# Block normalisation among the last six expert runs, and row-wise correction of the last four

## Chip, cores and metric

One core of one Trainium2 chip. Its engines run side by side, each through its own queue in program order: PE (matmul, with PEld for its weight loads), DVE (vector), ACT (activation functions), POOL (general, and the only issuer of row-indexed, that is indirect, DMAs here) and SP (issues plain DMAs). The metric is device time in microseconds. Three runs of the kernel before took 1161.5, 1162.44 and 1162.81 us; the median, 1162.44 us, is the time before.

## What is computed

The input is 32 sequences of 128 tokens, 256 wide (4096 tokens). A cross-attention with 16 heads is added to the tokens, then a mixture-of-experts layer: each token goes to the two best of eight experts, their results are weighed and summed, and a layer norm with gamma and beta is taken of token plus sum.

```python
    x = x + xattn(layernorm(x), ctx_768, ...)
    n = layernorm(x)
    # ffn(n):
    logits = n @ Wg + bg
    top2_vals, top2_idx = top_k(logits, 2)
    scores = softmax(top2_vals)
    y_e = gelu(n @ W1[e] + b1[e]) @ W2[e] + b2[e]
    out = sum over the two chosen e of scores_e * y_e
    x = x + layer_norm(n + out) * gamma + beta
```

## The kernel before

Everything is fp32. The tokens are eight blocks of 512. Attention runs block by block; `norm_gate` then writes a block's normed rows to DRAM twice: to `xrows`, from which the experts fetch, and to `total`, to which they add. Attention ends near 640 us of the span.

The expert layer is 43 runs (`MAIN`), each over 256 or 128 slots of one expert: 25 long and 18 short ones. A run's slots are tokens in order of their block, so early long runs hold tokens of early blocks. A list, `order`, says which run comes when: six long runs of tokens of the first four blocks (`AHEAD`, `OLD`), then short and long runs in turn, then two long runs (numbers 41 and 42) that hold no token of the first four blocks. A run m consists of

- `fetch_who(m)` (six runs ahead), `fetch_rows(m)` (four ahead, on POOL, one indirect gather for each 128 rows) and `fetch_weights(m)` (two ahead, on SP: W1 of 1 MB, a bias row, W2 of 1 MB, into one of three buffers);
- `turn(m)`: PE transposes the rows, DVE copies them out of PSUM;
- `hidden(m)`: eight times two matmuls (line 448), each pair followed on ACT by a Gelu (line 451);
- `outputs(m)`: for each 128 rows eight matmuls (line 466), two DVE steps (474 adds the bias, 475 multiplies by the score), and on POOL an indirect DMA that adds the rows to `total` (line 478). Such an add waits until the adds of the run before have landed.

In the loop PE works in the order hidden(m), turn(m+1), outputs(m-1). All results in PSUM, of whatever kind, take turns in eight banks. After run 40's first half stands a branch over three spare runs, which are not needed with these inputs (line 1179 waits for the register that decides it).

Then the ending. `outputs(40)`, the two transposes, and on SP the loads of the first four blocks' sums (line 1103) are issued; `hidden(41)`, `hidden(42)`, `outputs(41)`, `outputs(42)` follow. Those loads wait until run 40's add has landed; `declare_no_dep` with the list `early` keeps the adds of runs 41 and 42 from waiting for the loads. A block's norm is `measure` (DVE, four times lines 147 and 148, then 153, and a power on POOL, line 154), `scale` (a small DVE step, line 1129, then four activations on ACT, line 1131), `multiply` by gamma, which was copied to PSUM (line 1139), `add_residual` (line 1143) and `store`. Blocks 0 to 3 are normed beside the last two runs. Blocks 4 to 7 are loaded once run 42's adds have landed, and normed then. For two of them the residual was stored to the output earlier (line 1093), and the norm is added to it by DMA (line 1150).

Of the kernel before, what the change touches and what calls it, by code (L numbers as in the profile page):

```python
# [10 lines left out]
F32 = mybir.dt.float32  # L11
# [5 lines left out]
P = 128  # L17
# [8 lines left out]
def kernel(  # L26
# [38 lines left out]
    NPART = (2 * NTOK - NFULL * 256) // P + NE - 1  # L65


    OLD = NBLK // 2
    EARLY = (2 * OLD * TOK - NE) // 256 + NE


    AHEAD = 6
    assert AHEAD <= (2 * OLD * TOK - NE * 255 + 255) // 256
    SLOTS = 12 * CAP

# [36 lines left out]
    slots = dram.tile([SLOTS, 2], U32, name="slots")  # L112
    xrows = dram.tile([NTOK + P, D], F32, name="xrows")
    total = dram.tile([NTOK + P, D], F32, name="total")

    BW = NHC + D
    biases = dram.tile([NE, P, BW], F32, name="biases")
# [32 lines left out]
    def deviation(pool, mv, rstd):  # L150

        ve = pool.tile([P, TB], F32, name="ve", tag="ve")
        nc.vector.tensor_scalar_add(ve, mv[:, :, 1], LN_EPS)  # L153
        nc.gpsimd.tensor_tensor(rstd, ve, mhalf, ALU.pow)  # L154
# [298 lines left out]
                then()  # L453
        hiddens[m] = hT

    added, early = [], []

    def outputs(m, then=None):

        nt, who, hT = order[m][2], whos.pop(m), hiddens.pop(m)  # L460
        mine = []
        w1t, bt, w2t = weights.pop(m)
        for t in range(nt):
            py = flat(bank("py"))
            for c in range(NHC):
                nc.tensor.matmul(  # L466
                    py[:, :D],
                    lhsT=hT[c // (NHC // 2)][:, c % (NHC // 2), ts(t, P)],
                    rhs=w2t[:, c, :],
                    start=(c == 0),  # L470
                    stop=(c == NHC - 1),
                )
            y = f3.tile([P, D], F32, name=f"y{m}_{t}", tag="y")
            nc.vector.tensor_tensor(y, py[:, :D], bt[:, NHC:], ALU.add)  # L474
            nc.vector.tensor_scalar(y, y, who[:, t, 1:2].bitcast(F32), None, ALU.mult)  # L475
            if t > 0:
                nc.gpsimd.memset(apart, 0.0)
            add = nc.gpsimd.indirect_dma_start(  # L478
                out=reach(total, m),
                out_offset=bass.IndirectOffsetOnAxis(ap=who[:, t, 0:1], axis=0),  # L480
                in_=y,
                in_offset=None,
                compute_op=ALU.add,
            )


            for other in mine:
                tc.declare_no_dep(add.ins, other.ins, reason="tokens of their own")
            for other in added:
                tc.add_manual_dep(add.ins, other.ins.name, DATA, reason="the run before")  # L490
            if MAIN - 2 <= m < MAIN:
                for other in early:
                    tc.declare_no_dep(add.ins, other.ins, reason="no tokens of the first blocks")
            mine.append(add)
            if t == 0 and then is not None:
                then()
        added[:] = mine
# [583 lines left out]
    ADDED = (OLD, OLD + 1)  # L1081
# [12 lines left out]

    def load_sums(blk, n=1):

        tag = ("qT", "xnT", "rows", "wkm", "wvm")[blk // 2 if blk < 6 else blk - 3]
        acc = (a2 if blk < 6 else aw).tile([P, TB, D], F32, name=f"acc{blk}", tag=tag)
        accs[blk] = acc
        loads = []  # L1100
        for i in range(n):
            own = slice(blk * TOK + i * TOK // n, blk * TOK + (i + 1) * TOK // n)
            got = nc.sync.dma_start(  # L1103
                out=acc[:, ts(i, TB // n), :], in_=total[own, :].rearrange("(t s) d -> s t d", s=S)
            )
            for other in added:
                tc.add_manual_dep(got.ins, other.ins.name, DATA, reason="these sums are complete")
            loads.append(got)
        return loads

    def measure(blk, tiles=range(TB)):

        if blk not in scales:
            scales[blk] = (
                fs.tile([P, TB, 2], F32, name="mv3", tag="mv3"),
                fs.tile([P, TB], F32, name="rstd3", tag="rstd3"),
            )
        mv, rstd = scales[blk]
        for t in tiles:
            tile_stats(fs, accs[blk], mv, t)  # L1120
        if TB - 1 in tiles:
            deviation(fs, mv, rstd)

    def scale(blk):

# [9 lines left out]
    def multiply(blk, tiles=slice(0, TB)):  # L1135

        piece = accs[blk][:, tiles, :]
        w = piece.shape[1]
        nc.vector.tensor_tensor(piece, piece, factors[0].unsqueeze(1).to_broadcast([P, w, D]), ALU.mult)  # L1139

    def add_residual(blk, tiles=slice(0, TB)):
        piece = accs[blk][:, tiles, :]
        nc.vector.tensor_tensor(piece, piece, xres[blk][:, tiles, :], ALU.add)  # L1143

    def store(blk, tiles=slice(0, TB)):
        nc.sync.dma_start(out=of_block(out, blk)[:, tiles, :], in_=accs[blk][:, tiles, :])

    def send(blk):

        add = nc.gpsimd.dma_start(out=of_block(out, blk), in_=accs.pop(blk), accum_op=ALU.add)  # L1150
        tc.add_manual_dep(add.ins, stored[blk].ins.name, DATA, reason="the residual first")

    L = MAIN - 1
    pending = AHEAD - 1
    for m in range(AHEAD, L - 1):
        if m == L - 4:
# [10 lines left out]
        if m == L - 3:  # L1167
# [36 lines left out]
    measure(2)  # L1204
    scale(1)

    def third():
        measure(3)
        scale(2)

    def second():
        multiply(1)
        scale(3)
        multiply(2)

    outputs(L - 1, third)
    multiply(0)
    outputs(L, second)
    multiply(3)
    for blk in range(2):  # L1220
        add_residual(blk)
        store(blk)
    for blk in range(OLD, NBLK):
        load_sums(blk, TB if blk == OLD else 1)
    for blk in range(2, OLD):
        add_residual(blk)
        store(blk)
    measure(OLD)
    measure(OLD + 1, range(2))
    for blk in range(OLD, NBLK - 1):  # L1230
        scale(blk)
        measure(blk + 1, range(2, TB))
        if blk + 2 < NBLK:
            measure(blk + 2, range(2))
        multiply(blk)
        if blk in ADDED:
            send(blk)
    scale(last)
    add_residual(last - 1)
    store(last - 1)  # L1240
    for h in range(2):
        tiles = slice(h * TB // 2, (h + 1) * TB // 2)
        multiply(last, tiles)
        add_residual(last, tiles)
        store(last, tiles)


# [42 lines left out]
```

## Time and profile before

The profiled execution took 1161.17 us on the device; its trace spans 1159.5 us, so 1.7 us lie around the span. It is 1.3 us below the median of the runs shown.

| Engine | busy, us | share of the span |
|---|---|---|
| PE | 1110.3 | 96% |
| PEld | 859.2 | 74% |
| DVE | 585.3 | 50% |
| ACT | 462.5 | 40% |
| POOL | 288.7 | 25% |

| Costliest pieces of the expert layer | count | us of one |
|---|---|---|
| matmul of hidden, line 448 | 1376 | 0.336 (mean of both widths) |
| matmul of outputs, line 466 | 1088 | 0.379 |
| Gelu, line 451 | 344 | 0.429 |
| indirect add to `total`, line 478 | 68 | 1.666 |
| indirect gather of rows, line 419 | 64 | 0.988 |
| power on POOL, line 154 | 24 | 1.048 |

Matmuls overlap one another, so their durations add up to more than the time they take; the distance from one to the next is read from the timeline. A share of the whole span hides that stages differ: the time is looked at stage by stage.

### The profile page before, as it was taken

The numbers are of one execution on the slowest core, as the hardware profiler recorded it, in microseconds if no ns is written. First come the engines' busy times: TensorE is split into PE (matmuls) and PEld (weight loads), VectorE is DVE, ScalarE is ACT, GpSimd is POOL, SyncE is SP. The second block draws the span as 40 slices with busy tenths as digits, with TensorE's granted clock in tenths as the row PEclk, the third lists the DMA queues.
The fourth block names the chain that finished last, engine by engine and source line by source line (L and its number), as shares of the span: only waits on it lengthen the run. The fifth ranks groups of instructions, "written<-read, shape, count | busy, mean of one in ns | idle before, by whom it ended". The sixth has DMA issues, their size and how long they took to land. (4 is left out here: it accounts for less than half of the span.)

```text
span 1159.5 us, 19043 instructions
## 1 busy us (share of the span) xinstructions
PE 1110.3 (96%) x6805; PEld 859.2 (74%) x6805; DVE 585.3 (50%) x1476; ACT 462.5 (40%) x1609; POOL 288.7 (25%) x349
## 2 busy tenths in 40 slices
PE   7999999999999999999899999999999999999980
PEld 4666767676667676766668888899899898898870
DVE  4876685867867868678457361122211111111166
ACT  2565363544543635445244222333332332332252
POOL 1000012030030020300402563434433433433242
PEclk9999999999999999999899999999999999999995
DMA  9400101110111001001124758888888888888748
GB/s 311 146 1 19 38 1 19 37 20 1 38 19 38 1 2 37 2 1 39 19 78 133 224 111 271 245 248 239 261 241 259 240 243 244 266 247 259 203 107 220
DMA packets 124608, 148.59 MB, mean 128 GB/s; under 512 B 21536, under 2 KB 110048, under 8 KB 124512
## 3 DMA queue, kind: packets, MB, share of 16 engines
q1 hardware_dynamic: 107360, 127.35, 34.2%
q0 software_dynamic: 16160, 18.95, 8.8%
q8 instruction: 55, 0.90, 0.3%
q10 hardware_dynamic: 992, 1.05, 0.3%
q14 instruction: 41, 0.34, 0.1%
HBM read 122.97 MB, written 24.35 MB: 127 GB/s over the span
## 5 line engine op out<-in xcount | busy, mean ns | idle before, releaser
L451 ACT ACTIVATE hT<-ph,b 128x256 f32<-128x256 f32 (+1 forms) x344 | 146.4, 429 | 343.1 <-PE ph L448 306.0
L721 ACT ACTIVATE pr<-pss,nmax 128x128 f32<-128x128 f32 x512 | 179.2, 401 | 227.0 <-DVE nmax L717 215.8
L448 PE MATMUL ph<-xT,w 128*128 128x256 f32 (+1 forms) x1376 | 244.1, 336 | 0.6 <-DVE xT L436 0.6
L466 PE MATMUL py<-w,hT 128*128 128x256 f32 x1088 | 242.1, 379 | 1.0 <-DVEq L1179 1.0
L448 PEld LDWEIGHTS ph<-xT,w 128*128 128x128 f32 x1376 | 218.9, 191 | 22.5 <-DVE xT L436 0.9
L466 PEld LDWEIGHTS py<-w,hT 128*128 128x128 f32 x1088 | 203.4, 190 | 27.3 <-issue 1.4
L478 POOL DMA_INDIRECT total<-y,who x68 | 113.3, 1666 | 254.1 <-DVE y L475 173.6
L721 ACT ACTIVATION_READ_ACCUMULATOR pr<-pss,nmax 128x1 f32 x512 | 124.0, 242 | 0.0
L474 DVE TENSOR_TENSOR y<-py,b 128x256 f32<-128x256 f32 x68 | 28.9, 424 | 176.6 <-PE py L466 176.6
L686 PE MATMUL pq<-xnT,wq_sb 128*128 128x512 f32 x256 | 115.2, 592 | 0.3 <-DVE xnT L609 0.3
L780 PE MATMUL pw<-wo_sb,oT 128*128 128x256 f32 x512 | 113.3, 379 | 0.0
L436 DVE COPY xT<-px 128x512 f32<-128x512 f32 (+1 forms) x43 | 24.8, 578 | 169.0 <-PE px L434 165.7
L780 PEld LDWEIGHTS pw<-wo_sb,oT 128*128 128x128 f32 x512 | 96.0, 190 | 12.6 <-issue 0.2
L154 POOL TENSOR_TENSOR rstd<-ve,mhalf 128x4 f32<-128x4 f32 x24 | 25.1, 1048 | 282.5 <-DVE ve L153 279.4
L686 PEld LDWEIGHTS pq<-xnT,wq_sb 128*128 128x128 f32 x256 | 48.6, 190 | 61.3 <-issue 57.3
L128 POOL DMA_INDIRECT slots<-info,ati x64 | 62.8, 981 | 113.6 <-DVE ati L915 95.4
L735 DVE TENSOR_TENSOR pr<-pr,rden 128x512 f32<-128x512 f32 x128 | 88.5, 692 | 4.4
L717 DVE TENSOR_REDUCE nmax<-pss 128x4 f32<-128x512 f32 x128 | 79.4, 683 | 16.2 <-PE pss L707 16.2
L707 PE MATMUL pss<-kT,qT 64*128 64x128 f32 x1024 | 69.7, 282 | 5.3 <-issue 5.2
L707 PEld LDWEIGHTS pss<-kT,qT 64*128 64x128 f32 x1024 | 62.5, 190 | 12.5 <-issue 12.1
L745 PEld LDWEIGHTS ptp<-ident,pr 128*128 128x128 f32 x512 | 57.8, 141 | 17.0 <-issue 16.1
L419 POOL DMA_INDIRECT xg<-xrows,who x64 | 63.3, 988 | 22.5 <-issue 13.2
(164 smaller groups left out, 1147.1 us busy)
## 6 DMA issues: line engine op xcount, KB each, us to landing
w<-in_L_ffn_W_dram SPq DMA_DIRECT2D x86, 1024.0 KB
b<-biases SPq DMA_DIRECT2D x43, 132.0 KB
xres<-in_x_dram SPq DMA_DIRECT2D x8, 512.0 KB
xrows<-rows SPq DMA_DIRECT2D x8, 512.0 KB
total<-rows SPq DMA_DIRECT2D x8, 512.0 KB
acc<-total SPq DMA_DIRECT2D x7, 512.0 KB
ctx<-in_ctx_dram SPq DMA_DIRECT2D x8, 384.0 KB
out_dram<-acc SPq DMA_DIRECT2D x5, 512.0 KB
```

The source lines that it names most:

```text
L128: s = nc.gpsimd.indirect_dma_start(out=slots, out_offset=bass.IndirectOffsetOnAxis(ap=at, axis=0), in_=info, in_offset=None)
L419: nc.gpsimd.indirect_dma_start(out=xg[:, t, :], out_offset=None, in_=reach(xrows, m), in_offset=bass.IndirectOffsetOnAxis(ap=whos[m][:, t, ...
L448: nc.tensor.matmul(ph[:, : nt * P], lhsT=w1t[:, k, ts(c, P)], rhs=xT[:, k, :], start=(k == 0), stop=(k == KD - 1))
L451: nc.scalar.activation(hT[c // half][:, c % half, :], ph[:, : nt * P], AF.Gelu, bias=bt[:, c : c + 1])
L466: nc.tensor.matmul(py[:, :D], lhsT=hT[c // (NHC // 2)][:, c % (NHC // 2), ts(t, P)], rhs=w2t[:, c, :], start=(c == 0), stop=(c == NHC - 1),)
L478: add = nc.gpsimd.indirect_dma_start(out=reach(total, m), out_offset=bass.IndirectOffsetOnAxis(ap=who[:, t, 0:1], axis=0), in_=y, in_offse ...
L686: nc.tensor.matmul(pq, lhsT=wq_sb[:, k, ts(2 * q + c, P)], rhs=xnTs[blk][:, k, :], start=(k == 0), stop=(k == KD - 1),)
L707: nc.tensor.matmul(pss[2 * c + h][:, t, :], lhsT=qT[ts(h, DH), c, ts(t, S)], rhs=kT[ts(h, DH), c, ts(t, S)], start=True, stop=True,)
L717: nc.vector.tensor_reduce(nmax, pss[h], AX.X, ALU.max, negate=True)
L721: nc.scalar.activation(pr[:, t, :], pss[h][:, t, :], AF.Exp, bias=nmax[:, t : t + 1], accum_out=den[:, t : t + 1],)
L735: nc.vector.tensor_tensor(pr, pr, rden.unsqueeze(2).to_broadcast([P, TB, S]), ALU.mult)
L780: nc.tensor.matmul(pw[:, :D], lhsT=oTs[blk][:, k, ts(t, S)], rhs=wo_sb[:, k, :], start=(k == 0), stop=(k == NHP - 1),)
```

## The change

- `OLD` goes from 4 to 3 and `AHEAD` from 6 to 5. With these the list of runs becomes: five long runs, then 18 short and 14 long ones, then six long runs (37 to 42) without tokens of the first three blocks. The number of runs and their sizes stay. At the start of the mixed stretch two short runs precede each long one three times (runs 5 to 13).
- `fetch_rows(5)` and later ones move behind other steps, since run 5 is now one of the runs that the second table lists.
- Every block's residual (with beta) is stored to a new DRAM tensor `resid` (line 1093's place), where before two blocks' went to the output.
- The branch stands before run 37's first half. From run 37 (`X`) on PE works in the order hidden(m), turn(m+1), outputs(m).
- The sums of blocks 0 to 2 are loaded once run 36's add has landed, and those blocks are normed beside runs 37 to 39. The declaration with `early` is gone.
- The rows of `resid` that belong to the tokens of runs 39 to 42 are gathered on POOL (`fetch_own(bases, ...)`, eight indirect DMAs) beside run 38.
- The sums of blocks 3 to 7 are loaded once run 38's adds have landed, and normed and stored beside runs 39 to 42, still without the contributions of these runs.
- Runs 39 to 42 use `last_outputs`: the sums of the run's own tokens are gathered from `total` when the scatters of the run before have landed; DVE adds the run's result to them; the new sums are scattered over the rows of `total` (a plain write; not for run 42). `patch` norms these rows, multiplies by gamma and adds the residual rows; `send` scatters them over the stored rows of the output, after the stores of blocks 3 to 7 and after the rows of the run before.
- Gamma is read from SBUF instead of PSUM; `multiply`, `add_residual` and `store` become `by_gamma` and `put_out`.

```diff
-    OLD = NBLK // 2
+    OLD = 3
     EARLY = (2 * OLD * TOK - NE) // 256 + NE
...
-    AHEAD = 6
+    AHEAD = 5
...
+    resid = dram.tile([NTOK, D], F32, name="resid")
...
                 tc.add_manual_dep(add.ins, other.ins.name, DATA, reason="the run before")
-            if MAIN - 2 <= m < MAIN:
-                for other in early:
-                    tc.declare_no_dep(add.ins, other.ins, reason="no tokens of the first blocks")
...
     fetch_weights(2)
     norm_gate(last)
     fetch_rows(4)
-    fetch_rows(5)
...
     turn(4)
+    fetch_rows(5)
     outputs(2)
     fetch_weights(5)
     fetch_rows(6)
-    fetch_rows(7)
     hidden(4)
...
     fetch_weights(6)
+    fetch_rows(7)
     fetch_rows(8)
-    fetch_rows(9)
-    hidden(5)
-    turn(6)
-    outputs(4)
-    fetch_weights(7)
...
-        if blk in ADDED:
-            stored[blk] = nc.sync.dma_start(out=of_block(out, blk), in_=xres[blk])
-
-    def load_sums(blk, n=1):
+        nc.sync.dma_start(out=block(resid, blk), in_=xres[blk])
+    def load_sums(blk):
...
+        got = nc.sync.dma_start(out=acc, in_=block(total, blk))
+        for other in added:
+            tc.add_manual_dep(got.ins, other.ins.name, DATA, reason="these sums are complete")
+        return got
...
+    def by_gamma(rows):
+        w = rows.shape[1]
+        nc.vector.tensor_tensor(rows, rows, gamma_sb.unsqueeze(1).to_broadcast([P, w, D]), ALU.mult)
+    def put_out(blk):
+        acc = accs.pop(blk)
+        by_gamma(acc)
+        nc.vector.tensor_tensor(acc, acc, xres[blk], ALU.add)
+        stored[blk] = nc.sync.dma_start(out=of_block(out, blk), in_=acc)
+    PATCH = 4
     L = MAIN - 1
+    X = MAIN - (NREST - EARLY + AHEAD)
...
+    sums = aw.tile([P, PATCH, 2, D], F32, name="sums", tag="wo_sb")
+    bases = aw.tile([P, PATCH, 2, D], F32, name="bases", tag="wq_sb")
...
+    def own(t, m):
+        return t[:, m - (L - PATCH + 1)]
+    def fetch_own(t, table, m, complete=()):
+        for i in range(2):
+            got = nc.gpsimd.indirect_dma_start(
+                out=own(t, m)[:, i, :],
+                out_offset=None,
+                in_=table,
+                in_offset=bass.IndirectOffsetOnAxis(ap=whos[m][:, i, 0:1], axis=0),
+            )
+            for other in complete:
+                tc.add_manual_dep(got.ins, other.ins.name, DATA, reason="these sums are complete")
+    def last_outputs(m, then=None):
+        who, hT = whos.pop(m), hiddens.pop(m)
+        whose[m] = who
+        w1t, bt, w2t = weights.pop(m)
+        mine = []
...
+            y = f3.tile([P, D], F32, name=f"y{m}_{t}", tag="y")
+            z = own(sums, m)[:, t, :]
+            nc.vector.tensor_tensor(y, py[:, :D], bt[:, NHC:], ALU.add)
+            nc.vector.scalar_tensor_tensor(z, y, who[:, t, 1:2].bitcast(F32), z, ALU.mult, ALU.add)
+            if m < L:
+                if t > 0:
+                    nc.gpsimd.memset(apart, 0.0)
+                put = nc.gpsimd.indirect_dma_start(
+                    out=total,
+                    out_offset=bass.IndirectOffsetOnAxis(ap=who[:, t, 0:1], axis=0),
+                    in_=z,
+                    in_offset=None,
+                )
+                for other in mine:
+                    tc.declare_no_dep(put.ins, other.ins, reason="tokens of their own")
+                for other in added + loads:
+                    tc.add_manual_dep(put.ins, other.ins.name, DATA, reason="what came before")
+                mine.append(put)
+            if then is not None:
+                then(t)
+        added[:] = mine
+    def patch(m, tiles=slice(0, 2)):
+        z = own(sums, m)[:, tiles, :]
+        n = z.shape[1]
+        mv = fs.tile([P, 2, 2], F32, name="mvp", tag="mvp")
+        ve = fs.tile([P, 2], F32, name="vep", tag="vep")
+        rstd = fs.tile([P, 2], F32, name="rstdp", tag="rstdp")
+        for t in range(n):
+            tile_stats(fs, z, mv, t)
+        nc.vector.tensor_scalar_add(ve[:, :n], mv[:, :n, 1], LN_EPS)
+        nc.gpsimd.tensor_tensor(rstd[:, :n], ve[:, :n], mhalf[:, :n], ALU.pow)
+        for t in range(n):
+            nc.vector.tensor_scalar(z[:, t, :], z[:, t, :], mv[:, t, 0:1], rstd[:, t : t + 1], ALU.subtract, ALU.mult)
+        by_gamma(z)
+        nc.vector.tensor_tensor(z, z, own(bases, m)[:, tiles, :], ALU.add)
+    def send(m):
+        z = own(sums, m)
+        mine = []
...
+            put = nc.gpsimd.indirect_dma_start(
+                out=out_rows,
+                out_offset=bass.IndirectOffsetOnAxis(ap=whose[m][:, t, 0:1], axis=0),
+                in_=z[:, t, :],
+                in_offset=None,
+            )
+            for other in mine:
+                tc.declare_no_dep(put.ins, other.ins, reason="tokens of their own")
+            for other in sent + [stored[blk] for blk in range(OLD, NBLK)]:
+                tc.add_manual_dep(put.ins, other.ins.name, DATA, reason="over what came before")
+            mine.append(put)
+        sent[:] = mine
...
-        if m + WEIGHTS < L:
+        if m + WEIGHTS <= X:
             fetch_weights(m + WEIGHTS)
-        if m < L - 2:
+        if m < X - 1:
...
-    fetch_weights(L)
-    outputs(L - 2)
-    turn(L - 1)
-    turn(L)
+    fetch_weights(X + 1)
+    turn(X)
+    outputs(X - 1)
+    def run(m):
+        if m + WEIGHTS <= L:
+            fetch_weights(m + WEIGHTS)
+        if m + ROWS <= L:
+            fetch_rows(m + ROWS)
+        hidden(m)
+        if m < L:
+            turn(m + 1)
+    run(X)
     for blk in range(OLD):
-        early += load_sums(blk)
-    hidden(L - 1)
-    hidden(L)
-
-    pf = flat(bank("factors"))
-    nc.scalar.copy(pf[:, :D], gamma_sb)
-    factors = [pf[:, :D]]
-    measure(0)
-    measure(1)
-    scale(0)
-    measure(2)
+        load_sums(blk)
+    def behind_first():
+        measure(0)
+        measure(1)
+        scale(0)
+    outputs(X, behind_first)
+    for m in range(X + 1, L - PATCH):
+        run(m)
+        outputs(m)
+    for m in range(L - PATCH + 1, L + 1):
+        fetch_own(bases, resid, m)
+    m = L - PATCH
+    run(m)
+    put_out(0)
     scale(1)
 
...
+    def behind_second():
+        measure(2)
+        put_out(1)
         scale(2)
...
+    outputs(m, behind_second)
+    m = L - 3
+    fetch_weights(m + WEIGHTS)
     for blk in range(OLD, NBLK):
+        loads.append(load_sums(blk))
+    fetch_own(sums, total, m, added)
+    hidden(m)
+    turn(m + 1)
+    put_out(2)
+    measure(3)
+    def behind(t):
+        if t == 0:
+            measure(4)
+            scale(3)
+    last_outputs(m, behind)
+    put_out(3)
+    m = L - 2
+    fetch_own(sums, total, m, added)
+    fetch_weights(m + WEIGHTS)
+    hidden(m)
+    turn(m + 1)
+    measure(5)
+    scale(4)
+    measure(6)
+    scale(5)
+    put_out(4)
+    def behind(t):
+        if t == 0:
+            put_out(5)
+    last_outputs(m, behind)
+    measure(7)
+    m = L - 1
+    fetch_own(sums, total, m, added)
+    hidden(m, lambda: scale(6), 3)
+    turn(m + 1)
+    scale(7)
+    put_out(6)
+    patch(L - 3)
+    put_out(7)
+    last_outputs(m)
+    send(L - 3)
+    m = L
+    patch(L - 2)
+    fetch_own(sums, total, m, added)
+    hidden(m)
+    patch(L - 1)
+    send(L - 2)
+    def behind(t):
+        patch(L, slice(t, t + 1))
+        if t == 0:
+            send(L - 1)
+    last_outputs(m, behind)
+    send(L)
```

More of the change, by code (lines that the diff above doesn't have):

```diff
@@ L454, in hidden @@
         hiddens[m] = hT
-    added, early = [], []
+    added = []
     def outputs(m, then=None):
@@ L1071 @@
     fetch_weights(6)
+    fetch_rows(7)
     fetch_rows(8)
-    fetch_rows(9)
-    hidden(5)
-    turn(6)
-    outputs(4)
-    fetch_weights(7)
     accs, scales, stored = {}, {}, {}
-    ADDED = (OLD, OLD + 1)
     def of_block(t, blk):
@@ L1099, in load_sums, with measure @@
         accs[blk] = acc
[L1100 to L1117, printed above, removed]
+        got = nc.sync.dma_start(out=acc, in_=block(total, blk))
+        for other in added:
+            tc.add_manual_dep(got.ins, other.ins.name, DATA, reason="these sums are complete")
+        return got
+    def measure(blk):
+        scales[blk] = (
+            fs.tile([P, TB, 2], F32, name="mv3", tag="mv3"),
+            fs.tile([P, TB], F32, name="rstd3", tag="rstd3"),
+        )
         mv, rstd = scales[blk]
-        for t in tiles:
+        for t in range(TB):
             tile_stats(fs, accs[blk], mv, t)
-        if TB - 1 in tiles:
-            deviation(fs, mv, rstd)
+        deviation(fs, mv, rstd)
     def scale(blk):
@@ L1133, in scale @@
             )
[L1135 to L1146, printed above, removed]
@@ L1148, in send @@
-    def send(blk):
-        add = nc.gpsimd.dma_start(out=of_block(out, blk), in_=accs.pop(blk), accum_op=ALU.add)
-        tc.add_manual_dep(add.ins, stored[blk].ins.name, DATA, reason="the residual first")
-    L = MAIN - 1
+    def by_gamma(rows):
[6 more added lines that the diff above has]
+        stored[blk] = nc.sync.dma_start(out=of_block(out, blk), in_=acc)
@@ new lines @@
+    PATCH = 4
+    L = MAIN - 1
+    X = MAIN - (NREST - EARLY + AHEAD)
+    assert L - PATCH >= X + 1
+    out_rows = out.rearrange("b s d -> (b s) d")
+    sums = aw.tile([P, PATCH, 2, D], F32, name="sums", tag="wo_sb")
+    bases = aw.tile([P, PATCH, 2, D], F32, name="bases", tag="wq_sb")
+    whose, sent = {}, []
+    def own(t, m):
[10 more added lines that the diff above has]
+                tc.add_manual_dep(got.ins, other.ins.name, DATA, reason="these sums are complete")
@@ new lines, in last_outputs @@
+    def last_outputs(m, then=None):
[3 more added lines that the diff above has]
+        mine = []
+        for t in range(2):
+            py = flat(bank("py"))
+            for c in range(NHC):
+                nc.tensor.matmul(
+                    py[:, :D],
+                    lhsT=hT[c // (NHC // 2)][:, c % (NHC // 2), ts(t, P)],
+                    rhs=w2t[:, c, :],
+                    start=(c == 0),
+                    stop=(c == NHC - 1),
+                )
[11 more added lines that the diff above has]
+                    in_offset=None,
+                )
+                for other in mine:
[6 more added lines that the diff above has]
+        added[:] = mine
@@ new lines, in send @@
+    def send(m):
+        z = own(sums, m)
+        mine = []
+        for t in range(2):
+            if t > 0:
+                nc.gpsimd.memset(apart, 0.0)
+            put = nc.gpsimd.indirect_dma_start(
[3 more added lines that the diff above has]
+                in_offset=None,
+            )
+            for other in mine:
[4 more added lines that the diff above has]
+        sent[:] = mine
@@ L1154 @@
+    loads = []
     pending = AHEAD - 1
-    for m in range(AHEAD, L - 1):
-        if m == L - 4:
+    for m in range(AHEAD, X):
+        if m == X - 3:
             spare = nc.values_load(
@@ L1166 @@
             fetch_rows(m + ROWS)
-        if m == L - 3:
+        if m == X - 2:
             other = weights[m]
-        if m + WEIGHTS < L:
+        if m + WEIGHTS <= X:
             fetch_weights(m + WEIGHTS)
         hidden(m)
-        if m < L - 2:
+        if m < X - 1:
             turn(m + 1)
@@ L1205 @@
+    run(X)
+    for blk in range(OLD):
+        load_sums(blk)
[12 more added lines that the diff above has]
+    put_out(0)
     scale(1)
-    def third():
-        measure(3)
+    def behind_second():
+        measure(2)
+        put_out(1)
         scale(2)
[L1211 to L1222, printed above, removed]
-    for blk in range(OLD, NBLK):
[L1224 to L1245, printed above, removed]
+    outputs(m, behind_second)
+    m = L - 3
+    fetch_weights(m + WEIGHTS)
+    for blk in range(OLD, NBLK):
+        loads.append(load_sums(blk))
[8 more added lines that the diff above has]
+            scale(3)
```

## Prediction

> **What bounds the kernel now.** I read the page's slices first: PE is busy at nine tenths or more from the second slice to the 38th, so until the ending the kernel is as long as its matmuls. Then I cut the ending into stretches (columns: stretch, its length, busy time of PE, PEld, DVE, ACT, POOL with counts, granted PE clock, DMA share, GB/s):
>
> ```profile
> 1112.00:1126.60 14.60, 14.59 (x68) 12.51 (x66) 12.25 (x40) 8.77 (x18) 8.20 (x8) 1.00 0.23 45
> 1126.60:1159.50 32.90, 0.00 (x0) 0.00 (x0) 23.00 (x55) 9.00 (x18) 9.22 (x9) 0.54 0.82 200
> ```
>
> PE has no gap in the first stretch and no work in the second: 32.9 us of tail, in which DVE is busy 23 us. The chain of waits (start, us, what) says the same:
>
> ```profile
> 1098.70 14.08 PE L448 MATMUL ph<-xT,w 128*128 128x256 f32 x64 [0.63 <-DVE xT L436]
> 1112.78 13.83 PE py L466 x64
> ...
> 1127.72 3.83 DMA total<-y,who
> ```
>
> Two runs of matmuls, then the last add's landing, then loads and norms of blocks 4 to 7. The gain on offer is the tail; the price is whatever opens gaps in PE. Three views price that. First the timeline of the ending (start, us, engine, line; in brackets the idle time before and its releaser):
>
> ```profile
> 1101.91 1.55 POOL L478 DMA_INDIRECT total<-y,who  x1 [6.73 <-DMA total<-y,who]
> ...
> 1105.68 2.02 SPq L1103 DMA_DIRECT2D acc<-total  x4
> ...
> 1109.47 0.43 DVE L147 BATCH_NORM_STATS2 bnst<-acc 128x6 f32<-128x256 f32 x1 [10.23 <-DMA acc<-total]
> ...
> 1114.33 2.07 ACT L1131 ACTIVATE acc<-acc,shift,rstd 128x256 f32<-128x256 f32 x4 [0.77 <-DVE shift L1129]
> ```
>
> After run 40's matmuls end (1097.21), its add can issue only 4.7 us later, because the add before, issued at 1093.62, takes until 1101.9 to land. Then the new add lands (1105.68 starts the loads, +8.5), the first block arrives 3.8 us after its load's issue, and the next ones, by the DMA's busy stretch from 1107.3 to 1113.1 for four blocks, 1.5 us apart. A block's `measure` is 2.35 us of DVE (1109.47 to 1111.81), its `scale` 2.07 of ACT.
>
> Second, POOL's timeline in the loop:
>
> ```profile
> 803.67 2.35 POOL L478 DMA_INDIRECT total<-y,who  x1 [5.67 <-DVE y L475]
> ...
> 1040.14 1.62 POOL L478 DMA_INDIRECT total<-y,who  x1 [6.40 <-DVE y L475]
> 1042.07 0.98 POOL L419 DMA_INDIRECT xg<-xrows,who  x1 [0.30 <-PE ph L448]
> 1049.59 1.60 POOL L478 DMA_INDIRECT total<-y,who  x1 [6.54 <-issue]
> ...
> 1054.69 0.99 POOL L419 DMA_INDIRECT xg<-xrows,who  x1 [0.30 <-issue]
> ```
>
> An add lands 3.8 us after its issue when it is alone (1127.72), but the add of 1040.14 holds back the next one until 1049.59: 9.4 us beside a weight load. A gather takes 0.98 and 0.30 to the next: 1.28.
>
> Third, what a gap does to the clock. From 570 to 577 PE had gaps of 0.9 and 1.6 us, and the granted clock reads
>
> ```profile
> 573.00:574.00 1.00, 0.79 (x4) 0.51 (x4) 0.00 (x0) 0.00 (x0) 0.70 (x2) 0.50 0.53 172
> 582.00:583.00 1.00, 1.00 (x3) 0.56 (x3) 0.00 (x0) 1.00 (x8) 0.00 (x0) 0.58 0.00 0
> ```
>
> half from 573 until 582.8, and 1.00 after.
>
> **The change, part by part.**
>
> *Start and mixed stretch: nothing.* Rows of run 5 come one run later than they did, but its `turn` stands at 695.0, and its index row, issued first of six at 685.5, is there by about 688; a gather and its landing end by 692. It costs 1.3 us of POOL, hidden behind run 4's first half. The six residual stores more are 3 MB beside runs 9 to 16. Where two short runs precede a long one, three runs take 28.75 us of PE and ask for about 6.1 us of DMA each (2.2 MB at some 360 GB/s; the stretches from 1096 to 1102 read 308 to 389), 6 for four gathers and four adds (a lone add fills the DMA for 1.1 us, 1104 to 1105), and up to 6 for three stores (0.5 MB near 815 at 260 GB/s): about full. Only W1, the first 3 us of a load, is due when the first half starts, 10.9 us after the buffer is free (802.38 to 813.30). I take zero; the other end is 1 us in each of the three triples.
>
> *PE's own work: unchanged.* A long run is 6.9 (702.36 to 709.26) + 0.44 + 6.91 = 14.25. Run 37 starts where run 36 ends: 1097.2 - 4 x 14.25 + 0.4 (its transposes now stand ahead) = 1040.6. Times with a plus count from there. Six runs without a gap end at +85.1, that is 1125.7, as before (1126.6). The branch costs its 1.0 us as before.
>
> *Gap 1, run 38.* Run 36's add is issued at +4.5 and lands at +8.5 if it is alone. But the load of run 39's weights now follows 38's directly, so DMA is busy to about +11.7: between +8.5 and +13.9 (9.4 us), I take +12.6, near the loaded row. Blocks 0 to 2 land at +16.8, +18.3, +19.9. In the new order POOL has run 37's first add ahead of two powers, and with the `early` declaration gone it waits for all three loads: 1.9 + 2 x 1.05 brings rstd to +23. Queued behind it: on DVE the shift of block 0 and the bias add of run 37's last rows (+24.2; PE had them at +14.2), on ACT `scale(0)` to +25.5 and all Gelus of run 38. The last pair of matmuls of hidden(38) needs the bank that this bias add frees; PE is there at +20.3. Gap 3.7, then about 1.4 + 1.0 while `turn` and `outputs` wait for late Gelus: **6.1** (2.8 with the early landing).
>
> *Gap 2, run 39.* After run 37's second add (+26.3) POOL issues ten gathers, eight of residual rows and two of run 42's rows: 10 x 1.28 = 12.8. None was there before, and run 38's add and block 2's power queue behind them. [...] POOL is through at +40.9; add 1.9, power 1.05, shift, bias add: +44.7, where PE wanted the bank at +40.8. Gap 3.9 + 1.4 + 1.0 = **6.3** (4.1 at the low end).
>
> *Runs 39 to 41: small gaps, but DVE falls behind.* Run 38's second add is issued at +45.2 and lands at +49.6; the loads of blocks 3 to 7 land from +53.8 to +59.9 (5 x 1.5 after one another), and the scatter of run 39 waits for the last. A plain scatter of rows is not in the trace; its ends are the gather's 0.98 (line 419; 1.0 for line 128's scatter of short rows) and the add's 1.6. It is nearest to the first: 1.3 with what lies between, landing about 3 us (ends 2 and 3.8), more beside loads. Scatter, landing, two gathers, landing: the sums of run 40 are there at +74.8; powers 5 and 6 stand behind those gathers, so DVE gets shift 5 at +72. From there DVE has 22 us of work almost without a pause: four `put_out` at 2.3, block 7's `measure`, run 39's `patch` (3.3, and 1.6 for its power), copies, and four times bias and sum at 0.85. PE loses 0.9 + 1.3 + **4.0**, the last because half the Gelus of run 41 stand behind `scale(6)`. Its work ends at +104: gaps 18.8 in all.
>
> *The new tail.* DVE ends run 41's sums at +94.4. In series then: run 41's scatters (+97.3), run 39's rows to the output, which wait for block 7's store (+100.7), power, rest of `patch(40)` (+104.1), `patch(41)` (+109.0), first half of run 42 with its patch (+113.4), second (+118.0), two scatters, landing: +121.2. So the tail behind PE is 17 instead of 32.9.
>
> *Sum.* 1040.6 + 121.2 + 0.9 to close = 1162.7. Half-clock stretches after gaps 1 and 2 cost PE up to 3 us each, but they fall where PE would wait for POOL anyway; I add 0.7. Span 1163.4 against 1159.5: 15.9 won at the tail, 19.8 lost in gaps. With 1.7 around the span 1165.1 for the profiled execution's kind, with its 1.3 below the median 1166.4: **forecast 1166 us**.
>
> **The rivals.**
>
> *Short round trips (faster), 0.15.* [...]
>
> *No gaps at all, 0.06.* DVE and ACT work hides fully, the tail is one patch: 0.85 + 0.7 + 1.35 (power) + 1.4 + 2 x 1.3 + 3 = 10. 1125.7 + 11 = 1136.7, time **1140**. It needs the loads of blocks 0 to 2 before +17, against +8.5 for the load's issue alone.
>
> *Starved trips (slower still), 0.2.* Plain scatters cost as much as adds (1.9 with the pause, 3.8 to land), and gathers wait behind the 2.5 MB of loads: gaps 23.7, end +132.8, time **1177**.
>
> *The mixed stretch pays, 0.05.* DMA full in the triples, weights late: 3 us on top, **1169**.
>
> **How the numbers follow.** The forecast's case has 0.54 and reaches from 1160 to 1172. The range 1152 to 1177 takes in the low and high ends of landings, lock and scatters; only the gapless case and bad tails lie outside. A change under 0.2% (2.3 us) can't be told from none. Faster: 0.06 + 0.14, and little of the forecast's case: 0.2. Same (1160.1 to 1164.8): 0.16, mostly the forecast's lower part. Slower: 0.64.
>
> **What would show it.** Gaps of PE in runs 38 and 39, each with ACT's Gelus behind `scale`; POOL's ten gathers without a pause and run 38's add right after; a first scatter of run 39 released by the last load; a tail of 15 to 20 us made of POOL powers and scatters. If PE runs through to 1127, or the tail exceeds 25, I am wrong; likewise if a plain scatter takes 1.6 or lands after 6.

## Result, and the profile after

The changed kernel takes 1165.57 us (median of 18 runs, 1162.64 to 1169.97) beside 1162.53 us of the kernel before (18 runs): a ratio of 1.0029, 95% interval 1.002 to 1.0038. It is slower by 0.3%, about 3 us. The profiled execution took 1166.59 us, 1.0 above that median, with a span of 1164.9.

The ending first, in stretches cut as before (columns: stretch, length, busy time of PE, PEld, DVE, ACT, POOL with counts, granted clock, DMA share, GB/s). Changed kernel, stretches:

```profile
1135.60:1149.60 14.00, 14.00 (x65) 11.99 (x64) 8.85 (x23) 3.79 (x8) 8.87 (x11) 1.00 0.29 94
1149.60:1164.90 15.30, 0.02 (x1) 0.00 (x0) 6.93 (x18) 0.00 (x0) 7.30 (x11) 0.61 0.15 52
```

The tail behind PE has shrunk from 32.9 us to 15.3, and it is no longer bulk work: DVE and POOL are each busy for half of it and DMA for 15%, so it is a chain of small steps. But PE now ends at 1149.6 where it ended at 1126.6. The timeline of the changed kernel shows where that time went (start, us, engine, line; in brackets the idle time ahead and what ended it):

```profile
1055.13 1.47 SPq L1090 DMA_DIRECT2D acc<-total  x3
...
1059.00 0.43 DVE L148 BATCH_NORM_STATS2 bnst<-acc 128x6 f32<-128x256 f32 x1 [5.50 <-DMA acc<-total]
...
1062.56 1.62 POOL L479 DMA_INDIRECT total<-y,who  x1 [10.35 <-DVE bnst L148]
...
1063.61 2.63 POOL L155 TENSOR_TENSOR rstd<-ve,mhalf 128x4 f32<-128x4 f32 x2
...
1065.84 2.08 PE L449 MATMUL ph<-xT,w 128*128 128x256 f32 x4 [3.69 <-DVE y L475]
...
1084.96 1.13 PE L449 MATMUL ph<-xT,w 128*128 128x256 f32 x4 [1.88 <-DVE y L475]
...
1103.89 1.13 PE L449 MATMUL ph<-xT,w 128*128 128x256 f32 x4 [2.58 <-DVE y L1172]
...
1128.67 7.13 PE L1163 MATMUL py<-w,hT 128*128 128x256 f32 x24 [3.07 <-ACT hT L452]
```

Read the first four as one queue. POOL stands idle for 10.35 us with run 37's first add, which waits for the three loads; the trace puts the wait down to DVE's statistics, but the change made this add wait for the loads, and in the run below without that wait it issues 8.8 us earlier (+12.1 after run 37's start, here +20.9). Two powers follow it on POOL, and the bias add of run 37's second half, which stands on DVE behind the shift (the small DVE step of `scale`) that needs the first power, frees PE's bank only at 1065.8. The other PE rows are the same thing three more times: a bias add (L475, L1172) or the Gelus (L452), each behind the norm of some block. With three smaller ones (0.34, 1.00, 1.00) the gaps come to 13.6 us.

They are not the whole loss. The clock in the same kernel around the first gap, in stretches (the clock is the third figure from the end):

```profile
1062.00:1065.00 3.00, 0.15 (x1) 0.00 (x0) 1.63 (x7) 0.00 (x0) 2.44 (x3) 0.88 0.67 218
1065.00:1068.00 3.00, 2.11 (x5) 1.21 (x5) 0.86 (x3) 2.52 (x6) 2.77 (x4) 0.50 0.51 100
1068.00:1071.00 3.00, 3.00 (x9) 2.56 (x10) 1.85 (x2) 2.46 (x7) 2.09 (x4) 0.50 0.89 281
1071.00:1074.00 3.00, 3.00 (x15) 2.66 (x14) 1.70 (x3) 1.64 (x4) 2.39 (x3) 0.99 1.00 296
```

In the third row PE is busy throughout and gets through 9 matmuls, in the fourth through 15. From run 37's start to PE's end PE is busy 94.31 us here. In the run with two passes below, which has no gap there, it is 85.24 us for the same 405 recorded matmuls, so 9.1 us were lost beside the gaps. Three stretches ran at half clock, and in the fourth row the clock stayed up around run 39's two gaps:

```profile
1064.25:1071.08 6.83, 5.19 (x14) 3.84 (x15) 2.79 (x6) 4.98 (x12) 5.69 (x7) 0.50 0.69 175
1105.21:1112.03 6.82, 6.00 (x16) 4.95 (x17) 6.11 (x17) 4.17 (x11) 3.64 (x4) 0.50 0.48 139
1129.10:1132.51 3.41, 3.41 (x10) 2.73 (x9) 2.82 (x7) 2.56 (x6) 1.62 (x2) 0.50 0.48 150
1076.87:1094.49 17.62, 14.74 (x69) 12.39 (x68) 6.30 (x9) 4.98 (x12) 7.99 (x9) 1.00 0.70 203
```

PE was busy for 14.6 us at half clock, and half of that, 7.3 us, was lost to it. The other 1.8 us go with stopping and starting at the seven gaps, at any clock: in the fourth row PE is busy 14.74 us for one run, which takes 14.25 without a gap, so two stops cost 0.5.

### The profile page after: what moved, and what is told of

Same layout as the page of the kernel before. It is cut to its first block, busy times and chain, and to the rows that moved or that the text cites. A ratio compares the mean times of both kernels' runs of the same rounds, so it can differ in the third digit from the quotient of the medians.

```text
span 1164.9 us, 19129 instructions
## 1 busy us (share of the span) xinstructions
PE 1119.4 (96%) x6805; PEld 863.3 (74%) x6805; DVE 602.3 (52%) x1515; ACT 459.2 (39%) x1608; POOL 307.4 (26%) x377
## 5 line engine op out<-in xcount | busy, mean ns | idle before, releaser
L452 ACT ACTIVATE hT<-ph,b 128x256 f32<-128x256 f32 (+1 forms) x344 | 143.4, 430 | 304.7 <-PE ph L449 265.5
L467 PE MATMUL py<-w,hT 128*128 128x256 f32 x960 | 215.0, 381 | 0.0
L467 PEld LDWEIGHTS py<-w,hT 128*128 128x128 f32 x960 | 180.2, 191 | 23.0
L479 POOL DMA_INDIRECT total<-y,who x60 | 97.6, 1627 | 223.4 <-DVE y L476 121.2
L475 DVE TENSOR_TENSOR y<-py,b 128x256 f32<-128x256 f32 x60 | 25.4, 424 | 155.9 <-PE py L467 154.6
L778 PEld LDWEIGHTS pw<-wo_sb,oT 128*128 128x128 f32 x512 | 96.0, 190 | 12.6 <-issue 0.2
L705 PEld LDWEIGHTS pss<-kT,qT 64*128 64x128 f32 x1024 | 62.4, 190 | 12.6 <-issue 12.1
```

The source lines that it names most:

```text
L452: nc.scalar.activation(hT[c // half][:, c % half, :], ph[:, : nt * P], AF.Gelu, bias=bt[:, c : c + 1])
L467: nc.tensor.matmul(py[:, :D], lhsT=hT[c // (NHC // 2)][:, c % (NHC // 2), ts(t, P)], rhs=w2t[:, c, :], start=(c == 0), stop=(c == NHC - 1),)
L479: add = nc.gpsimd.indirect_dma_start(out=reach(total, m), out_offset=bass.IndirectOffsetOnAxis(ap=who[:, t, 0:1], axis=0), in_=y, in_offse ...
L705: nc.tensor.matmul(pss[2 * c + h][:, t, :], lhsT=qT[ts(h, DH), c, ts(t, S)], rhs=kT[ts(h, DH), c, ts(t, S)], start=True, stop=True,)
L778: nc.tensor.matmul(pw[:, :D], lhsT=oTs[blk][:, k, ts(t, S)], rhs=wo_sb[:, k, :], start=(k == 0), stop=(k == NHP - 1),)
```

## Experiments

Theory: POOL, DVE and ACT take their work in order; norm work that waits for late sums stands in front of bias adds and Gelus, which makes the PE gaps, and these with their half clock cost more than the shorter tail wins. Rivals: loads and landings at a full DMA set the end whatever PE does; or the loss is made ahead of the ending.

The kernels ran on several chips, on which the kernel before took 1145.6, 1145.8 and 1160.3 us. With the same code ahead of it, run 37 starts at 1024.3 to 1025.4 on the quicker ones and at 1039.6 to 1041.7 on the others. So I compare ratios to the kernel before on the same chip, and times from run 37's start in one profiled execution of each (a plus). All gaps are PE's, in us.

| run | gap in run 38 | in run 39 | later | PE ends | end | ratio, 95% interval |
|---|---|---|---|---|---|---|
| changed kernel | 3.69 | 1.88 + 1.00 | 7.0 | +107.9 | +123.2 | 1.0029 (1.002, 1.0038) |
| the same again | 3.32 | 1.75 + 1.00 | 10.2 | +112.0 | +126.8 | 1.0036 (1.0022, 1.005) |
| gathers early | 5.58 | 0 | 6.5 | +103.6 | +119.0 | 0.9999 (0.999, 1.0008) |
| norm behind | 0 | 10.33 | 7.0 | +107.1 | +122.6 | 1.0029 (1.0018, 1.0039) |
| both | 0 | 3.21 | 7.2 | +102.5 | +116.4 | 0.998 (0.9971, 0.9988) |
| no wait on loads | 0.69 | 4.25 | 7.0 | +103.2 | +118.5 | 1.002 (1.0007, 1.0032) |
| all behind | 0 | 0 | 4.7 | +91.9 | +115.7 | 0.9971 (0.996, 0.9981) |
| two passes | 0 | 0 | 0 | +85.2 | +107.8 | 0.9896 (0.9879, 0.9912) |

**Gathers early.** The first place is in the loop, where it holds for m = 34 to 36. Cut:

```diff
+        if L - PATCH + 1 <= m + WHO - 1 < L:
+            fetch_own(bases, resid, m + WHO - 1)
...
+    fetch_own(bases, resid, L)
     run(X)
...
-    for m in range(L - PATCH + 1, L + 1):
-        fetch_own(bases, resid, m)
```

> The eight gathers of residual rows are issued one pair per run, in runs 34 to 37, and no longer together in front of run 38's scatters. Theory (POOL's in-order queue holds the reciprocal deviation of block 2, and DVE's bias add of run 38 stands behind it): the gap of 1.88 + 1.00 us before run 39's last hidden tile goes, run 38's second bias add moves from +42.8 to about +38 after run 37's start, its scatter, the loads of blocks 3 to 7 and all behind them by about 5 us; the time falls by 3 to 6 us, to about 1161. Rival 1 (the loads and landings at a full DMA set the end, not PE): within 1 us of 1165.6. Rival 2 (the loss was made in the mixed stretch or before): within 0.5 us of 1165.6.

The gap in run 39 went (its bias add came at +40.1, not quite the +38), and against the changed kernel's ratio the time fell by 0.3% or 3.4 us, in the range forecast. The run also suggests that a gather is not free where it was moved to. Its timeline:

```profile
1031.17 0.42 DVE L475 TENSOR_TENSOR y<-py,b 128x256 f32<-128x256 f32 x1 [9.39 <-DMA total<-y,who]
...
1040.72 1.47 SPq L1090 DMA_DIRECT2D acc<-total  x3
...
1051.74 2.07 PE L449 MATMUL ph<-xT,w 128*128 128x256 f32 x4 [5.58 <-DVE y L475]
```

Run 36's bias add waits for an older add to land and give back its buffer, the loads of blocks 0 to 2 issue at +16.4 where they issued at +13.4, the gap in run 38 grew from 3.69 to 5.58, and run 37, which has no gap in the changed kernel, has one of 1.10. The run with both edits, with the same gathers there, has the late bias add too, and 0.45 in run 37; those are not in the table.

**Norm behind.**

```diff
     def behind_first():
         measure(0)
         measure(1)
-        scale(0)
-    outputs(X, behind_first)
+    outputs(X)
+    behind_first()
...
     run(m)
+    scale(0)
     put_out(0)
```

> The measuring of blocks 0 and 1 stands behind both bias adds of run 37, and the scaling of block 0 behind run 38's GELUs; the ten gathers stay where they are. Theory: the gap of 3.69 us in run 38's hidden stage and the half clock after it go, but POOL reaches block 2's reciprocal deviation no earlier than before (1082.7), so PE meets the same wait at run 38's second bias add, with a gap there of 6 to 9 us in place of 1.88: the time stays within 2 us of 1165.6. Rival (each PE gap is worth its own length and its own half clock): 5 to 7 us less, about 1159.5.

As the theory had it: the ratio is 1.0029 like that of the changed kernel. Its timeline at the next bias add:

```profile
1066.26 1.63 POOL L479 DMA_INDIRECT total<-y,who  x1 [0.30 <-issue]
1067.33 1.65 POOL L155 TENSOR_TENSOR rstd<-ve,mhalf 128x4 f32<-128x4 f32 x1
...
1069.56 2.07 PE L449 MATMUL ph<-xT,w 128*128 128x256 f32 x4 [10.33 <-DVE y L475]
```

PE came to run 39 without loss and waited there 10.33 us, more than the 6 to 9 expected, for the add and the power behind POOL's ten gathers. Taking away a wait ahead of a later one whose end another queue sets only moves it.

**Both of these.**

> Both edits of the two runs beside it: gathers spread over earlier runs, measuring behind the bias adds, scaling behind the GELUs. Theory: no PE gap and no half clock before run 40; run 38's second bias add at about +34 in place of +42.8, the loads of blocks 3 to 7 about 9 us earlier, the time about 1156 to 1158. More than the sum of the two alone, because the second gap takes up what the first frees. Rival (loads and landings set the end): 1164 or more.

The sum of the two alone is 0.3%, together they bring 0.5%: the second gap did take up what the first freed. But it is 5.6 us and not 8 to 10. A gap of 3.21 stays in run 39 (bias add at +38.2, not +34): two blocks' output steps, the measuring of block 2 and the wait for its power still stand ahead of it on DVE. The rival's 1164 or more (a ratio of 1.0013 or more) is out.

**No wait on loads.** The adds of runs 37 and 38 are declared independent of the loads of blocks 0 to 2, as the last two runs were before the change.

> The scatter-adds of runs 37 and 38 no longer wait for the loads of blocks 0 to 2 (those runs hold no tokens of these blocks), as it was in the kernel before; nothing else is changed. Theory: run 37's first scatter leaves POOL about 9 us earlier, so block 0's reciprocal deviation follows its variance at once; the bias add of run 37's second half comes 1.4 us earlier (the gap of 3.69 falls to about 2.3) and POOL's later queue about 2 us earlier; the time about 1163 to 1164. Rival (the wait for the blocks' statistics on DVE, not POOL, holds the bias add): within 0.5 us of 1165.6.

The bias add came 8.90 us after the issue of the loads (+10.51 to +19.41) where it took 10.24 (+13.44 to +23.68): the 1.3 us that the theory had given to POOL's queue, and now it follows DVE's statistics at once. The gap fell further than forecast (0.69) because in this execution the loads themselves issued 2.9 us earlier, behind an earlier add that the edit does not touch. Run 39 took most of it back (4.25 for 2.88). In time it is 0.1%, 1 us, and the intervals overlap: not shown to be different from the changed kernel. Its runs spread from 1143.7 to 1150.6, and the profiled one (1145.1) is among the quicker.

**All behind.** Residual rows gathered in runs 32 to 35 (with the index rows fetched two runs earlier for it), the declaration above, and the ending re-ordered by one rule: norm work stands behind bias adds and Gelus. `behind_second` had stood between the halves with measure(2), put_out(1) and scale(2). Two places, cut:

```diff
-    outputs(m, behind_second)
+    scale(0)
+    outputs(m)
+    put_out(0)
+    measure(2)
...
-    hidden(m, lambda: scale(6), 3)
+    hidden(m)
     turn(m + 1)
+    scale(5)
+    scale(6)
```

> A re-ordered ending with the same work: residual rows are gathered in runs 32 to 35; the scatter-adds of runs 37 and 38 do not wait for the loads of blocks 0 to 2; every measuring, scaling and output step of a block stands behind the bias adds of the run that it stood in front of, and every scaling behind a run's GELUs. Theory (in-order queues behind late sums make the PE gaps and the half clock after them, and both are worth their length at the end): no PE gap over 1 us from run 37 on, PE's last matmul about 90 us after run 37's start in place of 107.8; then DVE's backlog sets the end, with the last patch some 104 us after that start and the end at about 110 in place of 123.2: the time about 13 us under that of the changed kernel, a ratio to the kernel before of 0.990 to 0.993. Rival (landings at a full DMA and the chain of scatter, gather, scatter set the end whatever PE does): a ratio of 0.998 or more, as in the run with both edits.

Half right. PE has one gap left and ends at +91.9, 16 us earlier than in the changed kernel. The end came 7.5 us earlier, not 13, and the ratio of 0.9971 (interval 0.996 to 0.9981) is nearer to the rival's 0.998 than to the theory's 0.990 to 0.993. Its waits tell which of the two it is (engine, line, what it waited for: us in total, times, longest):

```profile
DVE sums L1207 <- POOL rstdp L1205: 8.2, 5, 2.5
...
PE py L1166 <- DVE y L1175: 4.7, 1, 4.7
...
DVE sums L1176 <- DMA sums<-total,who: 4.2, 1, 4.2
```

DVE, now the late engine, stood 8.2 us in the patches for POOL's powers and 4.2 us for run 40's sums, with a bias add that PE needed behind them. That can be taken out without touching a landing, and so tells the theory from the rival.

**Two passes.** A patch is split: `begin` takes the statistics and POOL's power, `finish` scales (on ACT for runs 39 to 41), multiplies by gamma and adds the residual rows, and another patch or block stands between. In runs 39 to 42 both bias adds stand ahead of both sums. The blocks' norm steps beside runs 39 to 41 were laid out anew with it. Cut:

```diff
-    def patch(m, tiles=slice(0, 2)):
+    def begin(m, tiles=slice(0, 2)):
...
+        marks[m, tiles.start] = z, n, mv, rstd
+
+    def finish(m, tiles=slice(0, 2), act=True):
...
+    begin(L - 2)
     fetch_own(sums, total, m, added)
...
+    finish(L - 3)
+    finish(L - 2)
+    begin(L - 1)
     send(L - 3)
```

> The ending of the run before (everything behind the bias adds) with DVE's own waits taken out: in runs 39 to 42 both bias adds stand in front of both sums, and each patch is split in two (statistics and POOL's power first, normalising later, the subtraction and scaling of runs 39 to 41 on ACT), so that DVE works on one patch while POOL holds another. Theory (in the run before, PE ended 15 us earlier but the end came only 7.5 us earlier, because DVE's backlog and its waits for POOL, some 8 us in the patches and 4.2 us for run 40's sums, set it): the end at about 105 after run 37's start in place of 115.7, a ratio to the kernel before of 0.987 to 0.991. Rival (the chain of scatter, landing, gather and of the ordered scatters of the result sets the end): a ratio of 0.996 to 0.998, no better than the run before.

The theory's number: 0.9896 (four runs), 1.0% under the kernel before and 1.4% under the changed one on the same chip (1148.34 us beside 1164.35), with the same blocks, runs and patches. The stretches of this run:

```profile
1110.80:1124.80 14.00, 14.00 (x66) 12.00 (x64) 8.97 (x23) 5.97 (x12) 7.51 (x9) 1.00 0.36 117
1124.80:1147.40 22.60, 0.04 (x1) 0.00 (x0) 8.20 (x25) 1.09 (x2) 11.28 (x16) 0.61 0.18 58
```

PE runs without a gap at full clock until 1124.8. The tail is longer again (22.6 us), and the chain of waits of this run says of what (start, us, what):

```profile
1074.41 10.88 DMA acc<-total
...
1118.58 1.06 POOL total L1186
1119.94 2.40 DMA total<-sums,who
...
1123.13 1.02 POOL sums L1147
...
1127.15 1.05 POOL out_dram L1241
1128.51 2.76 DMA out_dram<-sums,who
...
1132.06 0.96 POOL out_dram L1241
1133.32 2.44 DMA out_dram<-sums,who
...
1138.35 2.39 DMA out_dram<-sums,who
...
1141.59 0.96 POOL out_dram L1241
```

Here the rival's mechanism holds the end: four ordered pairs of scatters, three of which wait for the landing of the pair before (2.39 to 2.76 us). The chain of the changed kernel's end has one such landing (2.40). Further up, the chain of this run also has 10.88 us for the first of the loads of blocks 3 to 7, issued right behind run 41's weights. Both bound what is left (sending run 39's rows ahead of run 42's gathers was not tried, nor letting run 39's scatter go ahead of the loads of blocks 3 to 7, which would write rows while they are read, nor loading these blocks ahead of the weights).

**The start alone.** The kernel before with `AHEAD = 5`, the rows of runs 5, 7 and 9 fetched later, and all eight residual blocks stored beside the two that it stores; its ending is untouched.

> The kernel before, its ending untouched, with the changed kernel's start (5 runs prepared instead of 6, the rows of runs 5, 7 and 9 fetched later) and, beside the two blocks that it stores already, all eight residual blocks stored to a tensor of their own. Theory (the loss is made in the ending): a ratio of 0.999 to 1.001. Rival (the start and the residual traffic cost a third of it or more): 1.001 to 1.003, with run 41's start about 1 to 3 us later.

Ratio 1.0005 (0.9995 to 1.0014). The start and the stores cost nothing that shows; up to 1.6 us isn't excluded. `OLD` stays 4 here, so short and long runs alternate and the changed kernel's two short runs ahead of a long one are not in this run. The two traces of the first comparison settle that part. The same run's `hidden` behind attention starts, in the kernel before and in the changed one, at

```profile
642.97 7.07 PE L448 MATMUL ph<-xT,w 128*128 128x256 f32 x32
644.24 7.07 PE L449 MATMUL ph<-xT,w 128*128 128x256 f32 x32
```

That is 1.27 us later, ahead of everything that was changed in the order of runs, and run 37 starts 1.1 us later than I had worked out. Between the two nothing was lost.

**The changed kernel again**, beside the run with two passes.

> The changed kernel as it is, beside the run above on the same chip, so that its stretch from run 37's start to the end and its gaps can be compared on one chip. Both theories: a ratio to the kernel before of 1.002 to 1.004, and 121 to 124 us from run 37's start to the end, if the chip changes only what lies ahead of the ending.

The ratio is as forecast. The end at +126.8 lies outside: gaps in runs 40 and 41 are 3 us longer than in the first profile, and the profiled execution (1168.48) is 4.1 us above its median. The ten times run from 1161.8 to 1168.9. I take the spread to come from in-order queues that depend on when transfers land, which no run here shows by itself. Single figures past run 39 are good to some 3 us.

## Why the prediction was right, and where it was not

| step | predicted | measured |
|---|---|---|
| run 37 starts | 1040.6 | 1041.7 |
| loads 0 to 2 issue, block 0 there | +12.6, +16.8 | +13.4, +17.3 |
| run 37's second bias add | +24.2 | +23.7 |
| gap 1 | 3.7 + 1.4 + 1.0 | 3.69 |
| POOL through its ten gathers | +40.9 | +40.0 |
| run 38's second bias add | +44.7 | +42.8 |
| gap 2 | 3.9 + 1.4 + 1.0 | 1.88 + 1.00 |
| loads 3 to 7 issue, block 3 there | +49.6, +53.8 | +52.0, +55.6 |
| later gaps | 6.2 | 7.0 |
| half clock and stops | 0.7 | 9.1 (7.3 of it half clock) |
| PE ends | +104 | +107.9 |
| tail | 17 (18 by its own times) | 15.3 |
| end | +122.8 | +123.2 |

The mechanism was right in its main steps: no cost in the mixed stretch, two gaps made by POOL's queue, small ones after, a tail of POOL's powers and scatters. The two edits that aimed at a gap removed that gap, and the second confirmed that POOL's ten gathers stand behind the next one. 1166 against 1165.57 is closer than the terms deserve, and that part is luck: run 37 started 1.1 later, gaps were 5.2 shorter, half clock and stops 8.4 longer, the tail some 3 shorter, which leaves 1.5 of span; and the profiled execution, which I had put 1.3 below the median as in the kernel before, was 1.0 above it. Three sums of the prediction don't come out as written: the gaps add up to 18.6 (it has 18.8), the tail is 18 by its own times, and rstd of gap 1 comes at +23.9 (it has +23, but goes on from the right one). Term by term:

- *Half clock: 0.7, and it was 7.3, with 1.8 for the stops.* The "up to 3 us each" came from no row; the three stretches cost 2.6, 3.0 and 1.7. I argued that it falls where PE would wait for POOL anyway. For gap 2 that holds: PE came to it later, so it shrank from 6.3 to 2.9. But the clock also fell after the gaps of runs 40 and 41, where no later gap of PE waited for POOL: that is 4.7 of the 7.3.
- *The waits of 1.4 + 1.0 after gap 1 did not show.* They were worked out at full clock; at half clock PE took 2.08 us for four matmuls (1.13 after gap 2), and the Gelus kept up with it. After gap 2, at full clock, 1.00 showed. So gaps are 13.6 and not 18.8, and gaps, half clock and stops together 22.7 where I had 19.5.
- *Run 38's second add* took 8.1 us to land (1085.59 to 1093.65), not 4.4: the weights of run 41 were under way. It is the loaded row that I had shown, and I had taken the lone one.
- *The plain scatter*, which no row showed, is 0.95 to 1.06 us to issue where no DVE step lies beside it, 1.3 with its pause, as taken. It lands after 2.4 us when alone (1155.74; I took 3) and about 5 beside the loads of run 42's weights (1108.01 to the next gather at 1113.20).
- *POOL beside DVE (the lock of the range).* +40.9 is +26.3 + 12.8 and 1.8 for what POOL would lose beside DVE's steps, a term that no run shows: beside the ten gathers it lost 0.6, and POOL was through 0.9 earlier. What it lost is seen in single rows, a DVE step and the POOL operation beside it, first of the kernel before, then of the changed kernel:

```profile
803.31 1.22 DVE L1089 TENSOR_TENSOR xres<-xres,beta_sb 128x1024 f32<-128x1024 f32 x1
803.67 2.35 POOL L478 DMA_INDIRECT total<-y,who  x1 [5.67 <-DVE y L475]
...
1076.82 1.22 DVE L1119 TENSOR_TENSOR acc<-acc,gamma_sb 128x1024 f32<-128x1024 f32 x1
1077.27 1.58 POOL L1144 DMA_INDIRECT bases<-resid,who  x1 [0.30 <-issue]
```

The add, 1.6 us elsewhere, began 0.36 us into the step and lost 0.75 of the 0.86 that was left. The gather lost 0.63 (its neighbours take 0.95) with 0.77 of the step to go. With two passes an add of 2.31 us (1069.40) began 0.37 us into a step of line 1122 (1069.03, 1.22 us) and lost 0.7 with 0.85 to go. So where POOL lost time it lost most of what was left of the step. But gathers of the changed kernel that began 0.01 to 0.02 us ahead of a step (1069.71, 1071.00) took 0.98 and 0.95 and lost nothing, so not every meeting counts.

The rival with fast round trips (1155, with adds that land in 3.8 us beside loads too) failed at its landings: 8.1 us beside weight loads. The starved one (1177) failed at the plain scatter's price. The gapless one (1140) describes what the run with two passes does at PE, but had one patch in its tail where there are four ordered ones. The costly mixed stretch (1169) did not come: nothing was lost between 644 and run 37.

## What to carry to other kernels

Before work is laid beside a saturated engine, list for each in-order queue what stands directly behind every instruction that may wait; whatever frees PE's banks goes ahead of it, even if the waiting work then comes later. Shortening one wait is worth only the distance to the next one held by another queue, so look for that before pricing it. A PE gap of some 3 us is to be priced with the half clock after it: here 13.6 us of gaps brought 7.3 us of half clock and 1.8 us more for the stops.

## What I had not expected of the hardware

How long a gap is felt. In the changed kernel the granted clock was 0.50 from 1064.25 to 1071.08, from 1105.21 to 1112.04 and from 1129.10 to 1132.52, that is for 6.83, 6.83 and 3.41 us, after gaps of 3.69, of 2.58 and 1.00, and of 3.07. The starts of these stretches lie 40.96 and 23.89 us apart, 12 and 7 times 3.41. In attention of the kernel before it was 0.50 for 10.24 us (572.59 to 582.83).

The length of a gap alone doesn't decide. Run 39's gaps of 1.88 and 1.00 in the changed kernel left the clock at 1.00; in attention of the kernel before, gaps of 0.92 and 1.61 close together halved it (the prediction's rows). In five runs PE waits 4.74 us ahead of the last 24 matmuls of `outputs(41)`. At a clock of 1.00, 24 matmuls of this size take 5.34 us (1094.49 in the changed kernel, line 449); behind that gap they took 6.88 (norm behind), 7.08 (gathers early), 7.13 (no wait on loads), 7.66 (the changed kernel again) and 8.49 (both). So the price was 1.5 to 3.2 us on top of one and the same gap; what sets it, no run here shows.

The landing of an indirect scatter is not one number: 2.4 us for plain rows at the end, about 5 beside weight loads, 8.1 for an add beside weight loads.
